# A conditional layer with a mixture of experts on one core: zero rows stored one unit later, row loads of single slots on another queue, and another order of one pair's sums

## The chip, the cores and the metric

The kernel is written for Trainium2 and runs on one core of one chip. A core has a matrix engine (TensorE, PE in the profile; PEld are its weight loads), a vector engine (VectorE, DVE), an engine for activation functions (ScalarE, ACT), a general engine (GpSimd, POOL) and a sequencer that here only issues transfers (SyncE, SP). Each engine works through its own instructions in program order and waits on semaphores for what others produce. Transfers (DMAs) are issued by SP, ACT and POOL; 16 DMA engines carry them out.

The metric is the device time of one execution in microseconds (us), lower is better. Before the change three runs gave 1175.25, 1177.22 and 1178.05 us, a median of 1177.22.

## The reference

Two layers with a residual each, all in float32. Eight blocks of 512 tokens (4 batches of 1024), 512 features.

```python
def _L0_cond_ref(Efou, y, weight):          # y: one condition vector per batch
    scale = 1.0 / np.sqrt(np.float32(weight.shape[0]))
    ys = y * scale
    d = rsqrt(einsum('bi,io->bo', ys * ys, weight * weight) + EPS)
    return einsum('bsi,io->bso', Efou * ys[:, None, :], weight) * d[:, None, :]

def _L1_cond_ref(x, t_emb, router_W, router_bias, w1, w3, w2, W1e, W2e):
    D, HS, HE, E, K = (512, 1024, 512, 8, 2)
    shared = silu(xf @ w1) * (xf @ w3) @ w2
    s = sigmoid(concatenate([xf, tf], axis=-1) @ router_W)
    _, topk_idx = top_k(s + router_bias, K)
    s_sel = take_along_axis(s, topk_idx, axis=1)
    gates = s_sel / (s_sel.sum(axis=1) + 1e-09)
    combine = zeros((N, E)).at[arange(N)[:, None], topk_idx].add(gates)
    h = gelu(einsum('nc,ech->enh', xf, W1e), approximate=False)
    y = einsum('enh,ehc->enc', h, W2e)
    routed = einsum('ne,enc->nc', combine, y)
    return (shared + routed) / 3

x = x + _L0_cond_ref(x, cond, L0_weight)
x = x + _L1_cond_ref(x, cond, ...)
```

The kernel computes only the two experts that each token has chosen: 8192 pairs of a token and an expert.

## The kernel before

**First layer.** For each of the eight blocks the kernel multiplies by the modulated weights (L450), adds the residual, and stores the result x1 in HBM as rows (`turn_back`, L356, through `store_segments` on SP, L130). The stores of the last two blocks are the last transfers ahead of the second layer.

**Units of the second layer.** From there on work is a list of units that are run one after the other. Each unit first begins its own products, then in `rest` interleaves its further products with the second half (`parts`) of the unit before. The list holds:

- 24 units `Shared`: six blocks, four pairs of 128 hidden features each (`HU` is 4), for the shared network;
- 12 units `Double`: each handles two slots at once. A slot is 256 rows (`GS`) that all go to one expert; a pair of slots shares one expert's weights;
- 8 units `Slot`: single slots 24 to 31 (`SINGLE` is 24, `SURE` is 32). Behind them a `tc.Switch` (L1466) on the number of spare slots runs up to seven more single slots, from 32 on; in the run that is shown there are two;
- 8 units `Shared` for the last two blocks, beside which the experts' results are gathered and added to the output.

Most block products use a scheme with seven products instead of eight, which needs sums of blocks of both operands. VectorE makes these sums ahead of the products. `Double.sums_of_first` (L1022) makes four from the first expert matrix, called 1, 2, 7 and 4 by the product that uses them; `Double.sums_of_tokens` (L1000) makes those of the tokens, 3, 2, 1 and 4. A unit's products run in the order 1, 2, 6, 7, 5, 3, 4; product 6 takes weight sum 2 and token sum 2, product 7 takes weight sum 7 and token sum 3, product 5 weight sum 1 and token sum 1, product 3 weight sum 4, product 4 token sum 4.

**Tasks.** Work that isn't part of a unit's own chain hangs on a table, `tasks`: unit number `at` runs `tasks[2 * at]` after its value and gate have been multiplied, and `tasks[2 * at + 1]` at its end. The tasks that the change touches:

- `fill(i)` (L696): one DMA on SP that writes 768 rows of zeros into `x1s_d`, the HBM array of rows sorted by slot. 13 fills cover it. Two are appended to each of tasks 0 to 5 and one to task 6. Task 0 also holds `fetch_pairs(0)` (L687, L691), which loads the first block's rows of x1 into `base`; it is appended behind the two fills of that task.
- For the first `Double`: task `10 * HU + 6` makes its weight sums, task `10 * HU + 7` its token sums. Both are run by the last shared unit ahead of the pairs.

Routing runs on VectorE in tasks 3 to 9. From task 10 on POOL scatters token rows into `x1s_d` with indirect DMAs (L712); these need the zero rows to be there.

**Transfers of the slots.** Weights and rows of a slot come from HBM:

- `fetch_first(j)` (L964, issues at L968): expert matrix W1e of slot j as four DMAs of 256 KB on SP;
- `fetch_second(j)` (L970, issue at L972): W2e, one DMA of 1 MB on SP;
- `load_rows(j)` (L978): the slot's 256 token rows from `x1s_d` as four DMAs of 128 KB, through `load_segments` (L121, issues at L125), on SP. There are three buffers for rows, used in turn;
- `turn_rows(j)` (L985): transposes them on VectorE;
- results go to `ys_d`, from the pairs on SP (L1196), from the single slots on ACT (L1318).

In a single slot's `rest` SP gets, in this order: the row load of slot j + 3, then (behind the last part of slot j - 1, next to whose store on ACT it stands) the second matrix of slot j + 2, then the first matrix of slot j + 3. Single slots use three sets of weight buffers in turn.

SP therefore works through the stores of x1, the fills and base loads, then the weights, rows and stores of the pairs, and the weights and rows of the single slots, strictly in that order. POOL issues the indirect DMAs and the transfers of the last stage.

Of the kernel before, what the change touches and what calls it, by code (L numbers as in the profile page):

```python
# [30 lines left out]
ALU = mybir.AluOpType  # L31
# [5 lines left out]
GS = 256  # L37
# [8 lines left out]
def kernel(  # L46
# [14 lines left out]
    nc = tc.nc  # L61
# [16 lines left out]
    SINGLE = 2 * PAIRED  # L78
# [3 lines left out]
    early = NB - TAIL  # L82
# [30 lines left out]
    x1s_d = dram.tile([ROWS, D], FP, name="x1s_d")  # L113
# [7 lines left out]
    def load_segments(eng, tile_ap, dram_rows):  # L121

        v = dram_rows.rearrange("(q i) (g c) -> g i q c", i=Q, c=P)
        for g in range(KC):
            eng.dma_start(out=tile_ap[ts(g, Q)], in_=v[g])  # L125
# [51 lines left out]
    HU, KH, TH = HSC // 2, KC // 2, TB // 2  # L177
# [32 lines left out]
    for _ in range(WARM // 2):  # L210
# [5 lines left out]
        out=ident4, in_=ident4, compare_op=ALU.not_equal, fill=1.0, base=0, pattern=[[-1, B]], channel_multiplier=1  # L216
# [4 lines left out]
    for k in range(KC):  # L221
        nc.gpsimd.affine_select(
            out=fold[ts(k, Q)],
            in_=fold[ts(k, Q)],
            compare_op=ALU.not_equal,
            fill=1.0,
# [15 lines left out]
    for _ in range(WARM - WARM // 2):  # L242
# [10 lines left out]
        out=before, in_=before, compare_op=ALU.is_ge, fill=1.0, base=0, pattern=[[-1, P]], channel_multiplier=1  # L253
# [148 lines left out]
    def token_sum(blk):  # L402

        b = x1T[blk]
        nc.vector.tensor_tensor(b[:, :KH, HI], b[:, KH:, HI], b[:, :KH, HI], ALU.subtract)
        begun.add(blk)

    def token_sums(blk):
        b = x1T[blk]
        k1, k2 = slice(0, KH), slice(KH, KC)  # L410
        v = t_tiles[blk % 2].rearrange("p (n k t) -> p n k t", n=3, k=KH)
        t1, t2, t4 = (v[:, n] for n in range(3))
        sub = lambda o, i0, i1: nc.vector.tensor_tensor(o, i0, i1, ALU.subtract)
        if blk not in begun:
            token_sum(blk)
        nc.vector.tensor_tensor(t2, b[:, k1, HI], b[:, k1, LO], ALU.add)
        sub(t1, b[:, k2, HI], t2)
        sub(t4, b[:, k2, LO], t2)
        t_of[blk] = (t1, t2, b[:, k1, HI], t4)
# [5 lines left out]
    def weight_sums(u, matrices=(0, 1)):  # L425
        for i in matrices:
            s1, s2, s4 = s_views(i, u)
            a11, a12, a21, a22 = (
                w13[i][:, k, ts(2 * u + m, P)] for m in range(2) for k in (slice(0, KH), slice(KH, KC))
            )  # L430
            nc.vector.tensor_tensor(s1, a21, a22, ALU.add)
            nc.vector.tensor_tensor(s2, s1, a11, ALU.subtract)
            nc.vector.tensor_tensor(a21, a11, a21, ALU.subtract)
            nc.vector.tensor_tensor(s4, a12, s2, ALU.subtract)
# [261 lines left out]
    def fill(i):  # L696

        rows_z = x1s_d[ds(i * FILL, FILL)].rearrange("(s p) d -> p s d", p=P)
        nc.sync.dma_start(out=rows_z, in_=zeros.unsqueeze(1).to_broadcast([P, FILL // P, D]))
# [31 lines left out]
    def out_sums(u):  # L731
        t1, t2, t4 = out_tiles(u)
        b1, b2 = w2_sb[:, 2 * u, :], w2_sb[:, 2 * u + 1, :]
        b11, b12, b21, b22 = b1[:, LO], b1[:, HI], b2[:, LO], b2[:, HI]
        if u not in summed:
            nc.vector.tensor_tensor(b12, b22, b12, ALU.subtract)
            summed.add(u)
        nc.vector.tensor_tensor(t2, b12, b11, ALU.add)
        nc.vector.tensor_tensor(t1, b22, t2, ALU.subtract)
        nc.vector.tensor_tensor(t4, b21, t2, ALU.subtract)  # L740
# [214 lines left out]
    weights, rows, xg = {}, {}, {}  # L955
# [8 lines left out]
    def fetch_first(j):  # L964
        ev = expert(j)
        va = w1e.rearrange("e (g k j) h -> e g j k h", g=KC, k=KC, j=Q)
        for g in range(KC):
            nc.sync.dma_start(out=weights[j][0][ts(g, Q)], in_=va[ds(ev, 1), g][0])  # L968

    def fetch_second(j):  # L970
        ev = expert(j)
        nc.sync.dma_start(out=weights[j][1], in_=w2e.rearrange("e (k p) d -> e p k d", p=P)[ds(ev, 1)][0])  # L972

    def fetch_weights(j):
        fetch_first(j)
        fetch_second(j)

    def load_rows(j):  # L978
        rows[j] = later["xseg"][j % 3]
        load_segments(nc.sync, rows[j], x1s_d[ts(j, GS)])  # L980

    def turn_rows(j):
        xg[j] = later["xg"][j % 2]
# [3 lines left out]
    def turn_half(j):  # L987

        x = big[early - 2 + j // 2 % 2]
        for k in range(KC):  # L990
            nc.vector.transpose(x[:, k, ts(j % 2, GS)], rows[j][:, :, ts(k, Q)])

    class Double:
# [25 lines left out]
            w = weights[2 * self.j][0].rearrange("p k (q m c) -> p k q m c", q=2, m=2)  # L1019
            return [w[:, k, :, m, :] for m in range(2) for k in (slice(0, KH), slice(KH, KC))]  # L1020

        def sums_of_first(self):  # L1022
            a11, a12, a21, a22 = self.blocks()
            s1, s2, s4 = later["s_w"]
            nc.vector.tensor_tensor(s1, a21, a22, ALU.add)
            nc.vector.tensor_tensor(s2, s1, a11, ALU.subtract)
            nc.vector.tensor_tensor(a21, a11, a21, ALU.subtract)
            nc.vector.tensor_tensor(s4, a12, s2, ALU.subtract)

        def halves_of_second(self):  # L1030
            w = weights[2 * self.j][1].rearrange("p (q m) d -> p q m d", q=2)
# [57 lines left out]
        def rest(self, prev, task):  # L1089
# [9 lines left out]
            if following:  # L1099
                turn_half(2 * j + 2)  # L1100
                load_rows(2 * j + 5)
            else:
                turn_rows(SINGLE)
# [4 lines left out]
            if following:  # L1108
                turn_half(2 * j + 3)
                load_rows(2 * j + 6)  # L1110
# [87 lines left out]
    class Slot:  # L1198
# [26 lines left out]
        def rest(self, prev, task):  # L1225
            parts = [lambda mm=mm, drain=drain: (mm(), drain()) for mm, drain in prev.parts()]
            parts[0]()
            self.stage1(1)
            if self.j + 1 < self.end:
                turn_rows(self.j + 1)  # L1230
            if self.j + 3 < self.end and self.j != SURE - 1:
                load_rows(self.j + 3)
            self.blocks()
            self.row_sum()
            parts[1]()
            self.stage1(2)
            parts[2]()
            self.weight_sums()
            self.stage1(3)
            parts[3]()  # L1240
            if self.j + 3 < self.end and self.j not in (SURE - 2, SURE - 1):
                fetch_first(self.j + 3)
            task(2 * self.at)
            task(2 * self.at + 1)
# [140 lines left out]
    units = [Shared(blk, u) for blk in range(early) for u in range(HU)]  # L1385
# [7 lines left out]
    tasks = {i: [] for i in range(2 * len(units))}  # L1393
# [9 lines left out]
    for u, work in (  # L1403
        (0, [lambda: out_sums(0)]),
        (1, [lambda: weight_sums(3, (0,))]),
        (2, [lambda: weight_sums(3, (1,)), lambda: out_sums(1)]),
        (3, [sigmoid, pick_first]),
        (4, [pick_second]),
        (5, [lambda: out_sums(2), count]),
        (6, [across, slots_of_experts]),  # L1410
        (7, [lambda: out_sums(3), positions]),
        (8, [load_spare, gates]),
        (9, [norm_gates]),
        (8 * HU + 1, [lambda: fetch_weights(0)]),
        (6 * HU + 4, [open_slot_pools]),
        (10 * HU + 1, [lambda: fetch_first(2)]),
        (10 * HU + 4, [lambda: fetch_second(2)]),
        (10 * HU + 4, [lambda: turn_half(0), lambda: load_rows(3)]),
        (10 * HU + 5, [lambda: turn_half(1), lambda: load_rows(4)]),
        (10 * HU + 6, [lambda: units[early * HU].sums_of_first()]),  # L1420
        (10 * HU + 7, [lambda: units[early * HU].sums_of_tokens((3, 2, 1, 4))]),
        (2 * late, [reload_last, lambda: out_sums(0)]),
        (2 * late + 1, [lambda: out_sums(1)]),
        (2 * late + 3, [lambda: out_sums(2)]),
        (2 * late + 6, [lambda: out_sums(3)]),
        (2 * late - 1, [lambda: token_sum(early)]),
        (2 * late + 3, [turn_last]),
        (2 * late + 5, [lambda: token_sums(last_blk)]),
        (2 * (late + HU + 1), [reload_w2]),
    ):  # L1430
        tasks[u] += work
    for i in range((NSLOT - SURE) * SUB):
        tasks[6 * HU + 4 + i].append(lambda i=i: clear_rows(i))
    for i in range(ROWS // FILL):
        tasks[i // 2].append(lambda i=i: fill(i))
    for m in range(NT // 2):
        tasks[9 + 2 * m].append(lambda m=m: stage_rows(m))
        for i in range(2):
# [98 lines left out]
```

## Time and profile before

| what | value |
|---|---|
| median of three runs | 1177.22 us (1175.25 to 1178.05) |
| profiled execution, its own time | 1177.57 us |
| its span, first to last instruction | 1175.8 us |
| mean granted TensorE clock | 0.994 |
| bytes moved by DMA | 203.65 MB, 173 GB/s over the span |
| SP's and ACT's queues (q1, q10) | 45.6% and 3.6% of the 16 DMA engines' span |
| POOL's queue (q0) | 10.7% |

The stages of the span, read from the timeline of each engine:

| from (us) | stage |
|---|---|
| 27 | first layer, PE without a gap until 144.5 |
| 151 | shared units of six blocks; fills on SP from 145.9 to 194.7, scatter on POOL from 252 to 532 |
| 581 | pairs of slots |
| 863 | single slots; the branch to the spare ones at 980 |
| 1022 | shared units of the last two blocks, gather on POOL from 1028.6 |

The groups of DMA issues that matter here (line, queue, number, size, median time from issue to landing):

```profile
big<-in_L_cond_W1e_dram SPq DMA_DIRECT2D x88, 256.0 KB, 5.6
big<-in_L_cond_W2e_dram SPq DMA_DIRECT2D x22, 1024.0 KB, 5.5
x1s_d<-w0t SPq DMA_DIRECT2D x13, 1536.0 KB, 15.7
xsegs<-x1s_d SPq DMA_DIRECT2D x136, 128.0 KB, 4.2
```

The first two are expert weights, the third the fills, the last the row loads of all 34 slots. A group's time to landing holds what the transfer waits for others in the same queue.

How to read the lines of the profile: `L968` is line 968 of the kernel; `out<-in` names the tiles that an instruction writes and reads, buffer numbers left out. In a timeline the first two numbers are start and duration in us, and brackets give the engine's idle time before and what ended it. In a table of waits the numbers are total us, how many, and the longest. `SPq` and `ACTq` are the sequencers of SP and ACT, where DMAs are issued. Who ended a wait is inferred from semaphores; a wait for several is put down to the one that came last.

### The profile page before, as it was taken

What the parts mean: (1) busy time and instruction counts of PE and PEld (TensorE: products, weight loads), DVE (VectorE), ACT (ScalarE), POOL (GpSimd) and SP (SyncE); (2) the same over time, 40 slices, a digit from 0 to 9 for tenths busy, and PEclk for the clock granted to TensorE, in tenths of its full rate; (3) what the DMA queues carried; (4) which work ended last, traced back from release to release, by engine and by line L of the source; (5) the groups of instructions that cost most, each with busy time, mean ns of one, the idle gap of its engine ahead of it and who ended that gap; (6) DMA issues with size and microseconds to landing.
All of it is one profiled execution on the core that took longest, in us unless ns stands there. A gap on an engine that the chain in (4) does not pass through costs nothing.

```text
span 1175.8 us, 14158 instructions
## 1 busy us (share of the span) xinstructions
PE 1147.1 (98%) x5078; PEld 947.8 (81%) x5078; DVE 715.9 (61%) x1484; ACT 219.2 (19%) x395; POOL 156.9 (13%) x180
## 2 busy tenths in 40 slices
PE   8999989999999999999999999999999998999998
PEld 6444578888888888888888888888888887888886
DVE  4547647855455454553786776767635453469987
ACT  2000022111111111111122222222222211121111
POOL 2000000012121121210000000000000000087750
PEclk9999989999999999999999999999999998999999
DMA  9598499133322446335256677556775898188971
GB/s 173 112 231 201 98 369 373 37 111 123 125 90 99 152 153 209 139 138 152 54 126 161 168 205 182 160 147 191 196 195 152 212 232 221 56 252 290 307 265 71
DMA packets 148335, 203.65 MB, mean 173 GB/s; under 512 B 9876, under 2 KB 77588, under 8 KB 148248
## 3 DMA queue, kind: packets, MB, share of 16 engines
q1 hardware_dynamic: 123960, 148.01, 45.6%
q0 software_dynamic: 12864, 41.99, 10.7%
q10 hardware_dynamic: 11424, 12.59, 3.6%
q8 instruction: 42, 0.69, 0.3%
q14 instruction: 45, 0.37, 0.1%
HBM read 120.76 MB, written 81.79 MB: 172 GB/s over the span
## 4 chain that ended last, share of the span: by engine, by line
PE 85%; DMA 5%; DVE 5%; issue 1%; SPq 1%; ACT 1%; ACTq 0%; DVEq 0%; POOLq 0%; POOL 0%
PE ch L774 17%; PE s L910 14%; PE d L1170 12%; PE pl L450 8%; PE se L774 8%; PE chd L1066 7%; PE ph L1215 4%; PE tw L774 4%; PE sed L1066 3%; PE yc L1273 2%; PE twd L1066 2%; DMA ys_d<-yr 2%; PE yo L1273 2%; DMA big<-in_L_cond_W1e_dram 1%; DMA seg<-in_x_dram 1%
## 5 line engine op out<-in xcount | busy, mean ns | idle before, releaser
L1342 POOL DMA_INDIRECT big<-ys_d,addr x64 | 70.5, 1102 | 522.3 <-DVE addr L1341 507.1
L926 DVE SCALAR_TENSOR_TENSOR base<-s,base 128x512 f32<-128x512 f32 x131 | 88.7, 687 | 78.4 <-PE s L910 74.8
L910 PE MATMUL s<-w_sb,hgh 128*128 128x256 f32 x496 | 122.7, 380 | 1.9 <-DVE base L926 1.9
L450 PE MATMUL pl<-xT,wm 128*128 128x512 f32 (+1 forms) x288 | 117.0, 554 | 1.5 <-DVE xT L280 1.4
L712 POOL DMA_INDIRECT x1s_d<-big,addr x64 | 64.5, 1008 | 360.6 <-DVE addr L711 339.5
L819 ACT ACTIVATE hgh<-ch 128x512 f32<-128x512 f32 x96 | 57.3, 597 | 284.6 <-PE ch L774 267.0
L910 PEld LDWEIGHTS s<-w_sb,hgh 128*128 128x128 f32 x496 | 93.8, 190 | 16.2 <-DVE base L926 3.5
L450 PEld LDWEIGHTS pl<-xT,wm 128*128 128x128 f32 x288 | 52.4, 190 | 52.8 <-issue 46.9
L823 DVE TENSOR_TENSOR hgh<-se,hgh 128x512 f32<-128x512 f32 x64 | 44.0, 688 | 77.4 <-ACT hgh L819 67.7
L910 PE MATMUL s<-more,hgh 128*128 128x256 f32 x316 | 81.3, 380 | 0.9 <-DVE xsegs L926 0.9
L774 PE MATMUL ch<-w0t,seg 128*128 128x256 f32 x256 | 62.8, 389 | 7.5 <-ACT hgh L819 7.4
L1187 DVE TENSOR_TENSOR yd<-d,yd 128x512 f32<-128x512 f32 x36 | 24.8, 689 | 71.1 <-ACT yd L1183 38.7
L910 PEld LDWEIGHTS s<-more,hgh 128*128 128x128 f32 x316 | 59.9, 190 | 9.6 <-DVE xsegs L926 1.3
L1170 PE MATMUL d<-big,hgh 128*128 128x256 f32 x288 | 66.1, 379 | 0.0
L774 PEld LDWEIGHTS ch<-w0t,seg 128*128 128x128 f32 x256 | 49.3, 194 | 15.9 <-ACT hgh L819 9.2
L1170 PEld LDWEIGHTS d<-big,hgh 128*128 128x128 f32 x288 | 54.7, 190 | 7.4
L774 PE MATMUL ch<-t,seg 128*128 128x256 f32 x256 | 60.5, 379 | 0.0
L774 PEld LDWEIGHTS ch<-t,seg 128*128 128x128 f32 x256 | 48.6, 190 | 6.6
L774 PE MATMUL ch<-big,w_sb 128*128 128x256 f32 x224 | 53.3, 381 | 0.0
L774 PE MATMUL se<-big,w_sb 128*128 128x256 f32 x224 | 53.0, 379 | 0.0
L774 PE MATMUL tw<-big,w_sb 128*128 128x256 f32 x224 | 52.9, 379 | 0.0
L774 PE MATMUL ch<-big,seg 128*128 128x256 f32 x224 | 52.9, 379 | 0.0
(263 smaller groups left out, 1934.6 us busy)
## 6 DMA issues: line engine op xcount, KB each, us to landing
big<-in_L_cond_W1e_dram SPq DMA_DIRECT2D x88, 256.0 KB, 5.6
big<-in_L_cond_W2e_dram SPq DMA_DIRECT2D x22, 1024.0 KB, 5.5
x1s_d<-w0t SPq DMA_DIRECT2D x13, 1536.0 KB, 15.7
xsegs<-x1s_d SPq DMA_DIRECT2D x136, 128.0 KB, 4.2
ys_d<-yd SPq DMA_DIRECT2D x24, 512.0 KB, 4.3
x_d<-back SPq DMA_DIRECT2D x32, 256.0 KB, 4.7
big<-x_d SPq DMA_DIRECT2D x16, 512.0 KB, 3.7
base<-x_d SPq DMA_DIRECT2D x12, 512.0 KB, 5.4
```

The source lines that it names most:

```text
L450: nc.tensor.matmul(pas[oc][:, ds(lo, n)], lhsT=wms[b][:, k, oc, :], rhs=xTs[blk][:, k, ds(lo, n)], start=(k == 0), stop=(k == KC - 1),)
L712: ins = nc.gpsimd.indirect_dma_start(out=x1s_d, out_offset=bass.IndirectOffsetOnAxis(ap=at.bitcast(U32), axis=0), in_=staged(t // 2)[:, t ...
L774: nc.tensor.matmul(out, lhsT=lhs[:, k, :], rhs=rhs[:, k, :], start=start and k == 0, stop=k == KH - 1, skip_group_check=not start,)
L819: nc.scalar.activation(self.both[:, :, m, cols], self.chain, AF.Copy)
L823: nc.vector.tensor_tensor(r, bank, r, ALU.add)
L910: nc.tensor.matmul(out[:, s], lhsT=a[:, ts(s, P)], rhs=b, start=start and s == 0, stop=True, skip_group_check=not (start and s == 0),)
L926: nc.vector.scalar_tensor_tensor(r, bank, third, r, ALU.mult, ALU.add)
L1066: nc.tensor.matmul(bank[:, q], lhsT=lhs[:, k, q, :], rhs=rhs[:, k, :], start=start and q == 0 and k == 0, stop=k == KH - 1, skip_group_che ...
L1170: nc.tensor.matmul(out[:, i], lhsT=a[:, q, ts(i, P)], rhs=b[:, q, :], start=start and i == 0 and q == 0, stop=q == 1, skip_group_check=not ...
L1215: nc.tensor.matmul(self.ph[:, i], lhsT=weights[j][0][:, k, ts(c, P)], rhs=xg[j][:, k, :], start=(k == 0), stop=(k == KC - 1),)
L1273: nc.tensor.matmul(out, lhsT=a[:, k, :], rhs=b[:, k, :], start=start and k == 0, stop=k == HC // 2 - 1, skip_group_check=not start,)
L1342: nc.gpsimd.indirect_dma_start(out=picks[t][i], out_offset=None, in_=ys_d, in_offset=bass.IndirectOffsetOnAxis(ap=at.bitcast(U32), axis=0) ...
```

## The change

Three things are changed.

1. `fill(i)` is appended to `tasks[1 + i // 2]` instead of `tasks[i // 2]`: every fill runs one task, half a unit, later. The first two now stand in task 1 and the last one in task 7.
2. `load_rows(j)` issues on SP for slots below `SINGLE` (24) and on GpSimd's queue for all others. The pairs' calls reach up to slot 26, so the loads of slots 24, 25 and 26, called from the last pairs, change their queue too.
3. `sums_of_first` takes the names of the sums that it makes. For the first pair, weight sums 1 and 2 stay in task 46; task 47 then makes token sums 3 and 2, weight sums 7 and 4, token sums 1 and 4. For the later pairs the call is as before.

```diff
     def load_rows(j):
         rows[j] = later["xseg"][j % 3]
-        load_segments(nc.sync, rows[j], x1s_d[ts(j, GS)])
+        load_segments(nc.sync if j < SINGLE else nc.gpsimd, rows[j], x1s_d[ts(j, GS)])
...
-        def sums_of_first(self):
+        def sums_of_first(self, names=(1, 2, 7, 4)):
             a11, a12, a21, a22 = self.blocks()
             s1, s2, s4 = later["s_w"]
-            nc.vector.tensor_tensor(s1, a21, a22, ALU.add)
-            nc.vector.tensor_tensor(s2, s1, a11, ALU.subtract)
-            nc.vector.tensor_tensor(a21, a11, a21, ALU.subtract)
-            nc.vector.tensor_tensor(s4, a12, s2, ALU.subtract)
+            for n, (out, i0, i1, op) in {
+                1: (s1, a21, a22, ALU.add),
+                2: (s2, s1, a11, ALU.subtract),
+                7: (a21, a11, a21, ALU.subtract),
+                4: (s4, a12, s2, ALU.subtract),
+            }.items():
+                if n in names:
+                    nc.vector.tensor_tensor(out, i0, i1, op)
...
-        (10 * HU + 6, [lambda: units[early * HU].sums_of_first()]),
-        (10 * HU + 7, [lambda: units[early * HU].sums_of_tokens((3, 2, 1, 4))]),
+        (10 * HU + 6, [lambda: units[early * HU].sums_of_first((1, 2))]),
+        (10 * HU + 7, [lambda: units[early * HU].sums_of_tokens((3, 2))]),
+        (10 * HU + 7, [lambda: units[early * HU].sums_of_first((7, 4))]),
+        (10 * HU + 7, [lambda: units[early * HU].sums_of_tokens((1, 4))]),
...
     for i in range(ROWS // FILL):
-        tasks[i // 2].append(lambda i=i: fill(i))
+        tasks[1 + i // 2].append(lambda i=i: fill(i))
```

## The prediction

> **What bounds the kernel now.** I read the page's first part, then a table by stage, then TensorE's (PE's) timeline, and last the waits of SyncE's queue (SP).
>
> ```profile
> PE 1147.1 (98%) x5078; PEld 947.8 (81%) x5078; DVE 715.9 (61%) x1484; ACT 219.2 (19%) x395; POOL 156.9 (13%) x180
> ```
>
> PE is the bound: the span is 1175.8 us, so only 28.7 us can be won without taking matmuls away. The table by stage says where they lie (us; PE, PEld, DVE, ACT and POOL busy, then granted clock, DMA share and GB/s):
>
> ```profile
> 145.00:241.00 96.00, 87.68 (x395) 75.98 (x396) 68.20 (x167) 20.19 (x35) 0.00 (x0) 0.96 0.70 254
> 575.00:610.00 35.00, 33.00 (x151) 28.05 (x150) 29.76 (x54) 7.65 (x12) 0.00 (x0) 1.00 0.21 62
> 925.00:955.00 30.00, 27.23 (x125) 23.40 (x124) 15.45 (x35) 5.46 (x12) 0.00 (x0) 1.00 0.91 225
> 955.00:985.00 30.00, 25.44 (x118) 22.00 (x116) 12.77 (x28) 5.46 (x12) 0.00 (x0) 0.99 0.92 239
> 985.00:1020.00 35.00, 33.78 (x141) 28.69 (x142) 14.56 (x32) 6.62 (x15) 0.00 (x0) 0.91 0.38 117
> ```
>
> The holes belong to the three places of the change: shared work begins at 145 (fills), pairs begin at 575 (their sums), single slots run from 888 to 1021 (row loads). PE's timeline has the five gaps, each in brackets with what ended it:
>
> ```profile
> 151.01 3.78 PE L774 MATMUL ch<-w0t,seg 128*128 128x256 f32 x8 [6.47 <-ACT hgh L819]
> 585.82 1.96 PE L1066 MATMUL chd<-t,more 128*128 128x256 f32 x8 [1.62 <-DVE t L1007]
> 926.90 1.97 PE L1215 MATMUL ph<-xg,big 128*128 128x256 f32 x8 [1.51 <-DMA big<-in_L_cond_W1e_dram]
> 954.30 1.97 PE L1215 MATMUL ph<-xg,big 128*128 128x256 f32 x8 [1.26 <-DMA big<-in_L_cond_W1e_dram]
> 985.47 3.75 PE L1215 MATMUL ph<-xg,big 128*128 128x256 f32 x8 [5.03 <-DMA xsegs<-x1s_d]
> ```
>
> Two gaps cost more than their length: behind 6.47 and 5.03 eight matmuls take 3.78 and 3.75 us, behind the others 1.96 to 1.97. The trace's clock record has half clock from 148.32 to 155.15 and from 984.59 to 991.42. So the second loses another (991.42 - 985.47) / 2 = 2.97 us.
>
> In the single stage the weights come late, and SP's waits (total, times, longest) say why:
>
> ```profile
> SPq L968 <- DMA ys_d<-yr: 44.3, 5, 12.7
> SPq L972 <- DMA ys_d<-yr: 9.3, 1, 9.3
> ```
>
> A fetch of expert weights waits for a *store of results* that ScalarE (ACT) issued, though the two share no data. The trace's instructions show the link: SP's and ACT's DMAs raise eight semaphores in turn (100, 102, 104 to 109), and each waits for the DMA before it on the same one. The fetch of 27, begun at 889.10, stood at its third part until 903.07, when slot 24's store on semaphore 100 had landed (issued 900.03, landed 903.05). DMAs were meanwhile idle:
>
> ```profile
> 895.00:901.00 6.00, 6.00 (x29) 5.29 (x28) 3.75 (x8) 1.36 (x3) 0.00 (x0) 1.00 0.03 10
> 910.00:913.00 3.00, 3.00 (x16) 2.64 (x15) 2.28 (x5) 0.98 (x2) 0.00 (x0) 1.00 0.00 0
> ```
>
> So this stage is short of issue, not of bandwidth.
>
> **Fills one unit later.** The same 13 transfers; the first two no longer stand at 145.93 and 147.30 behind the stores of x1, but behind the two base loads (150.19, 150.60). The first eviction (L819) waits for the last of those stores: issued 144.68, landed 150.11. Stores in that row land 1.0 to 1.4 us apart (125.45, 126.84, 128.01, 129.17 undisturbed; 146.79, 148.02 here), the last 2.09, the only one with fills behind it. Without them: 148.02 + 1.2 = 149.2, 0.9 us sooner. But half clock lasts to 155.15 either way, so each microsecond of it is worth half: **-0.4** (0 to -0.9). What is late next: the fills begin up to 4.2 us later, the last lands at some 210 instead of 206.45. SP's next issue behind them is at 217.94, the first scatter into the filled rows at 252.3; both cover it, and with that cover gone up to 4.2 us would show. The base rows land some 9 us sooner than 162.3; their first use is at 170.29: nothing.
>
> **Sums for the first pair.** Eight DVE operations in both versions, none added. Before: four weight sums (L1025 to L1028, 578.16 to 580.77), the add L823, the product L871, four hidden sums, then tokens 3 (584.27) and 2 (584.98); PE waits for the latter. After, sums 7 and 4, each 0.60 us of pitch (579.49, 580.09, 580.69), come behind tokens 2. All between moves up 1.2 us: L823 may run at 579.49, as its bank is done at 579.0; L871 follows ACT at some 580.9. PE starts at 584.6 instead of 585.82: **-1.2** (0 to -1.6, the whole gap). Late next are sum 7, ready at 585.1 where its product starts at 586.3, and sum 4 and tokens 1 and 4, done at 586.9 as before. PE has no hole from 600 to 925, so it keeps this.
>
> **Row loads of slots 24 and up on POOL.** 10 loads of four DMAs leave SP: 40 issues of 0.45 us, 18 us of a queue off the path. On POOL such a 128 KB load does not occur; the nearest are SP's own (0.45 us, landing in 3.7) and POOL's four loads of 256 KB at 1038 (0.66 us each, landing in 7 to 9), so 1.8 to 2.7 us a slot. POOL does nothing from 531 to 1028, which covers them: they wait for the turn of the slot three before, and the last (33, behind the turn at 956.9) is through by 960, ahead of the first gather at 1028.64. The rows are needed two slots, 26 us, later, so 9 us to land is hidden; without that cover a turn of 1.42 us would be late. POOL now passes the branch on the number of spare slots at 960, not 530; its 4.3 us there are hidden too.
>
> What counts is the order left behind. A slot now takes 6 of the eight semaphores' turns instead of 10, so a fetch shares one with a store further back. In a slot's own order the eighth after a store is a fetch more than a slot later; even if stores keep their present place, some 14 of SP's DMAs early, a fetch waits for the store of the slot three before it. That one meets idle DMAs and lands in 3 us; the last of four 256 KB parts lands 1.5 + 4.6 us later (issue, median landing). At 9 of the 13 us between slots (900.03, 912.98), both gaps close: **-2.8** (0 to -3.1 with their restarts).
>
> The third gap is another thing, whatever the row says of a row load. PE's sequencer meets the branch at 978.19 and has its next instruction 6.8 us later, having run dry at 980.44; SP, DVE and ACT need 6.1 to 6.8 too, with DMAs full (share 1.0 to 1.25). POOL took 4.3 at 530, DVE 2.8 at the branch's end at 1022 (share 0.05, then 0.49). With the row load of 33 and the weights of 32 gone from that moment (2.3 MB were issued from 975.5 to 980), but the fetch of 33 now likely there, I take 4.8 us, nearer POOL's: the gap falls from 5.0 to 3.0. Half clock began 4.1 us into this gap and 3.8 into the first, so a gap of 3.0 ends before it: -2.0 - 3.0 = **-5.0** (0, fetch as slow as now, to -8.0, all of it). The Trainium skill, "TensorE: Matmul & The Clock Gate", Part 1, states a free-running idle window of about 3.4 us; by it too 3.0 us keeps the clock, but 3.5 may not, and the term would be near -1.5. No run here shows a gap of that size.
>
> Sum: -0.4 - 1.2 - 2.8 - 5.0 = -9.4 on the profiled execution's 1177.57 us (span 1175.8 and 1.8 around it): **1168.2 us**. That execution is 0.35 above the median of 1177.22, inside the runs' own spread of 2.8.
>
> **Rivals.** *The branch stays as slow*: the sum without its last term, 1173.2. For it: the fetch of 33 now reaches the branch's moment. Against: it is 1 MB, less than what lies there now.
>
> *The queue brings nothing*: fetches still stand behind stores, or the DMAs are simply full (share 0.92 at 955). Only the first two terms: 1176.0. Against: shares of 0.03 and 0.00 while SP waited. The Trainium skill, "DMA: Bandwidth & Descriptors", "Issuing engines are not separate DMA queues", speaks for it: another issuing engine saves the sequencer's time alone; by that rule the result is this rival's 1176.0. The trace disagrees in so far as SP lost 53.6 us to those two rows of waits.
>
> *Slower: the store lands late at every slot.* If fetches still wait for the store of three slots before, and the DMAs are full when it is issued, it needs the 7.5 to 8.0 us seen from 925.93 on; then 8.0 + 1.5 + 4.6 = 14.1 against 13.0: 1.1 us late at each of seven slots, 7.9 instead of 2.8. 1177.57 + 5.1 - 1.6 = 1181.1. It decides once a store takes over 6.9 us to land. Against: the rows are what made that moment full.
>
> *Better*: the branch's gap and half clock vanish: 1165.2.
>
> **How the numbers follow.** Forecast 0.46, slow branch 0.26, nothing 0.10, slower 0.11, better 0.07. The measurement tells about 0.2%, 2.4 us. Forecast, slow branch and better are faster by more, and so 0.79; nothing lies within it, 0.10; slower 0.11. The range from 1164.5 to 1176.5 takes in the bounds of the branch's term and the rival that brings nothing, and leaves out the slower one and a little below.
>
> **What would show it.** The first matmul at L774 after the stores some 0.9 us sooner; the wait at L1007 down to 0.4; no waits of L968 or L972 for ys_d stores over some 4 us, and no gap ended by a W1e load in the single slots; PE's gap at the branch near 3 us and only one stretch of half clock. It is wrong if the fetches of 27 to 33 still stand for 8 to 13 us, if the branch's gap stays at 5 us, or if POOL's row loads end a wait of DVE.

## The result and the profile after

| | before | after |
|---|---|---|
| median (five runs each) | 1176.28 us | 1167.09 us |
| lowest and highest | 1175.25, 1178.05 | 1166.89, 1170.75 |
| profiled execution, its span | 1177.57, 1175.8 | 1166.89, 1165.1 |

The ratio of the times is 0.9929, with a 95% interval from 0.9911 to 0.9947: between 6 and 10 us faster. The forecast was 1168.2 us.

Where the time came from is seen in the same views as before. First the busy time of each engine, from the first part of the page of the kernel after:

```profile
PE 1143.6 (98%) x5078; PEld 946.0 (81%) x5078; DVE 715.7 (61%) x1484; ACT 219.2 (19%) x395; POOL 181.3 (16%) x220
```

PE has the same 5078 matmuls and 3.5 us less busy time, which is half clock gone. POOL has 40 instructions more, the row loads. The table by stage (length; busy PE, PEld, DVE, ACT, POOL; then granted clock, DMA share, GB/s), at roughly the places that correspond:

```profile
143.30:239.30 96.00, 88.41 (x406) 76.67 (x405) 68.45 (x168) 20.19 (x35) 0.00 (x0) 0.96 0.71 258
573.00:608.00 35.00, 34.20 (x157) 29.10 (x156) 30.57 (x55) 7.98 (x13) 0.00 (x0) 1.00 0.23 69
893.00:923.00 30.00, 30.00 (x140) 26.41 (x139) 15.96 (x35) 6.83 (x15) 4.61 (x8) 1.00 0.92 239
923.00:953.00 30.00, 30.00 (x140) 26.41 (x139) 16.75 (x39) 5.84 (x13) 4.61 (x8) 1.00 0.93 245
950.00:980.00 30.00, 27.06 (x126) 23.54 (x125) 13.12 (x30) 5.46 (x12) 0.00 (x0) 1.00 0.77 222
974.00:1009.00 35.00, 31.32 (x144) 26.61 (x142) 15.39 (x34) 6.71 (x16) 0.00 (x0) 1.00 0.23 78
```

The first of the three rows for the single slots has its counterpart in this row of the kernel before:

```profile
895.00:925.00 30.00, 30.00 (x140) 26.41 (x139) 15.73 (x34) 6.83 (x15) 0.00 (x0) 1.00 0.55 140
```

PE is now busy for all of 923 to 953, where it had 27.23 of 30 us; the row from 950 on holds the gap at the branch, and has 27.06 where it had 25.44. The DMAs' share in the three stretches was 0.55, 0.91 and 0.92 and is now 0.92, 0.93 and 0.77: the transfers come earlier, and less of them is left for the branch. From the branch on (974) the clock is 1.00 instead of 0.91. PE's timeline has three of the five gaps left:

```profile
150.03 3.53 PE L774 MATMUL ch<-w0t,seg 128*128 128x256 f32 x8 [5.26 <-ACT hgh L819]
583.17 1.97 PE L1070 MATMUL chd<-t,more 128*128 128x256 f32 x8 [0.41 <-DVE t L1007]
977.48 1.97 PE L1219 MATMUL ph<-xg,big 128*128 128x256 f32 x8 [2.94 <-issue]
```

Both gaps that ended with a W1e load are gone. The first has shrunk by 1.21 us, the second by 1.21, the one at the branch by 2.09, and its eight matmuls take 1.97 us instead of 3.75. Up to the last two microseconds of the span the clock record has one stretch of half clock, from 146.34 to 153.17. Added up: 1.2 (first gap) + 0.5 (half clock behind it, which cost (155.15 - 151.01) / 2 = 2.07 us and now (153.17 - 150.03) / 2 = 1.57) + 1.2 + 2.8 (two W1e gaps) + 2.1 + 3.0 (branch and its half clock) = 10.8 us. The spans differ by 10.7.

SP's waits in the single slots, from 886 to 986 us (total, times, longest):

```profile
SPq L968 <- DMA ys_d<-yr: 26.3, 4, 7.5
SPq L972 <- PE yc L1277: 25.5, 7, 8.8
```

Fetches still wait for stores, half as long, and the other wait is for the buffer that PE frees, as it should be. So something of the old order is left, and the runs below had to show whether it costs anything.

### The profile page after: what moved, and what is told of

Its sections match the earlier page's. It is cut to its first block, busy times and chain, and to the rows that moved or that the text cites. A ratio compares the mean times of both kernels' runs of the same rounds, so it can differ in the third digit from the quotient of the medians.

```text
span 1165.1 us, 14183 instructions
## 1 busy us (share of the span) xinstructions
PE 1143.6 (98%) x5078; PEld 946.0 (81%) x5078; DVE 715.7 (61%) x1484; ACT 219.2 (19%) x395; POOL 181.3 (16%) x220
## 5 line engine op out<-in xcount | busy, mean ns | idle before, releaser
L125 POOL DMA_DIRECT2D xsegs<-x1s_d x40 | 23.2, 588 | 388.3 <-DVE big L991 296.5
```

## The experiments

Three runs make one part of the change each. The others test the mechanism behind the third part, then what is left.

**One part at a time.** Fills alone:

```diff
-        tasks[i // 2].append(lambda i=i: fill(i))
+        tasks[1 + i // 2].append(lambda i=i: fill(i))
```

> The kernel before with the fills one unit later and nothing else. Theory (the last store of x1 lands sooner, half clock eats half of it): that store lands some 1.0 us sooner, the gap before the first eviction falls from 6.47 to 5.3 to 5.5 us, time 0.4 to 1.7 us below the kernel before, the branch's gap stays near 5 us. Rival (the fills' late end costs something before the scatter): a wait for a fill appears near 250 us and the time is not lower.

Measured 1175.82 us against 1177.27, ratio 0.9986 (0.9977 to 0.9994): 0.7 to 2.7 us, 1.6 in the middle, more than the 0.4 of the forecast. The first gap in the timeline of this kernel:

```profile
150.13 3.78 PE L774 MATMUL ch<-w0t,seg 128*128 128x256 f32 x8 [5.68 <-ACT hgh L819]
```

PE starts 0.88 us sooner, because the last store of x1 landed at 149.23 instead of 150.11, as worked out. The last fill landed at 208.23 and no instruction waited for one. The half clock here lasted from 145.89 to 156.13; it does not end "at 155.15 either way".

Sums alone (`sums_of_first` as in the diff of the change, and its two calls):

```diff
-        (10 * HU + 6, [lambda: units[early * HU].sums_of_first()]),
-        (10 * HU + 7, [lambda: units[early * HU].sums_of_tokens((3, 2, 1, 4))]),
+        (10 * HU + 6, [lambda: units[early * HU].sums_of_first((1, 2))]),
+        (10 * HU + 7, [lambda: units[early * HU].sums_of_tokens((3, 2))]),
+        (10 * HU + 7, [lambda: units[early * HU].sums_of_first((7, 4))]),
+        (10 * HU + 7, [lambda: units[early * HU].sums_of_tokens((1, 4))]),
```

> The kernel before with the new order of the first pair's sums alone. Theory: PE's gap at the first product with token sum 2 (1.62 us before) falls to 0.4, time 1.2 us below, nothing else moves. Rival (the four sums pushed back stop a later product): a new gap of up to 1 us within the first pair, time within 0.4 us of the kernel before.

Measured 1174.85 us, ratio 0.9981 (0.9973 to 0.9990): 1.2 to 3.2 us. Two lines of its timeline:

```profile
584.33 1.97 PE L1070 MATMUL chd<-t,more 128*128 128x256 f32 x8 [0.42 <-DVE t L1007]
926.04 1.97 PE L1219 MATMUL ph<-xg,big 128*128 128x256 f32 x8 [2.13 <-DMA big<-in_L_cond_W1e_dram]
```

The gap is the 0.42 us of the whole change; the W1e gaps stay, the first even longer than before (2.13). The gap accounts for 1.2 of the 2.2 us in the middle of that interval. In the profiled execution more was won at the branch, which this part does not touch: a gap of 4.58 us and half clock of 3.41 us behind it, against 5.03 and 6.83 before. The fills' execution had 4.66 and 3.41 there. The branch of the kernel before thus differs from one execution to the next by itself.

Row loads alone:

```diff
-        load_segments(nc.sync, rows[j], x1s_d[ts(j, GS)])
+        load_segments(nc.sync if j < SINGLE else nc.gpsimd, rows[j], x1s_d[ts(j, GS)])
```

> The kernel before with the row loads of slots 24 and up on GpSimd's queue alone. Theory: this part carries most of the change. Both gaps that a first-matrix fetch ended (1.51 and 1.26 us) go, the branch's gap falls from 5.0 to about 3 and its half clock goes: 7 to 8.5 us below the kernel before. Rival (the branch's time is chance and does not follow the load on the DMAs): only 2.8 us below, with the branch at 5 us and half clock behind it.

Measured 1170.66 us, ratio 0.9943 (0.9931 to 0.9956): 5.2 to 8.1 us, most of the whole. No W1e gap is left. Of the branch's gap a larger part stays than after:

```profile
981.06 3.54 PE L1215 MATMUL ph<-xg,big 128*128 128x256 f32 x8 [3.95 <-issue]
```

Behind it there is half clock for 3.41 us (980.85 to 984.27). Before had 6.83, but the fills alone and the sums alone had 3.41 there too, so this is not shown to come from the row loads.

In the middle of their intervals the three parts add up to 1.6 + 2.2 + 6.7 = 10.5 us; the whole change brought 8.4 (6.2 to 10.5). Within these errors they agree.

**Is it the shared semaphores, or the row loads' bytes and issues?** This kernel is the one before, with the row loads left on SP. Only the ten stores of the single slots change their queue, from ACT's to POOL's:

```diff
-            nc.scalar.dma_start(out=as_pair(ys_d, j * GS), in_=self.pair)
+            nc.gpsimd.dma_start(out=as_pair(ys_d, j * GS), in_=self.pair)
```

> The kernel before, its row loads still on SP, but the stores of the single slots' results on GpSimd's queue instead of ScalarE's. The same bytes, and SP issues as much as before. Theory (a fetch stands behind a store because both raise the same eight semaphores in turn): SP's waits for stores of results, 53.6 us in the single slots, vanish, both gaps ended by a first-matrix fetch (2.8 us) close, and the time falls by 2.8 us or more, up to 7.8 if the branch also gets quicker. Rival (the row loads on SP themselves, by their issue time or their bytes, make the weights late): both gaps stay and the time is within 1 us of the kernel before.

Measured 1170.02 us, ratio 0.9937 (0.9924 to 0.9949), as much as the row loads' move brings. Its SP waits, then SP's timeline at the fetch of 28 with the row load behind it:

```profile
SPq L972 <- PE yc L1273: 31.9, 7, 5.9
SPq L125 <- DMA big<-in_L_cond_W2e_dram: 7.1, 5, 2.1
```

```profile
900.45 1.99 SPq L968 DMA_DIRECT2D big<-in_L_cond_W1e_dram  x4
902.54 3.90 SPq L125 DMA_DIRECT2D xsegs<-x1s_d  x4
```

No wait for a store of a single slot (ys_d<-yr) is left. SP still issues every row load, 2.9 to 3.9 us of its time per slot, and the same bytes are moved; yet the fetch of 28, which began at 917.09 before, is out at 902.44, and both W1e gaps are gone. What cost the time was that a fetch stood behind a store on the same semaphore, not the row loads themselves. The branch's gap came down too, to 2.91 us: SP issues the last row load ahead of the branch, which before stood at 976.97 to 978.82, at 954.23 to 957.14 here.

**What the waits that are left cost.** The same edit on the kernel after:

> The changed kernel with the stores of the single slots on GpSimd's queue too. In the changed kernel SP's fetches still wait 26.3 us for stores of results, but no gap of PE is left that a fetch ended. Theory (those waits are now hidden, only the semaphores' sharing makes them): they vanish, and the time stays within 2 us of the changed kernel, 9 us below the kernel before. Rival (the late fetches still cost something at the branch, because they lie on the DMAs there): the branch's gap falls from 2.9 to 1.5 us or less, time 1 to 3 us below the changed kernel.

Measured 1168.30 us (1166.45 to 1170.8), ratio 0.9923 (0.9908 to 0.9938): no different from after, 0.9929. Its SP waits in the single slots, and PE's gap at the branch:

```profile
SPq L972 <- PE yc L1277: 51.9, 7, 9.0
```

```profile
978.45 1.96 PE L1219 MATMUL ph<-xg,big 128*128 128x256 f32 x8 [2.63 <-issue]
```

The 26.3 us of waits for stores have turned into waits for the buffer (25.5 to 51.9), and the time stayed: they were hidden.

**What makes the branch slow.** The forecast's largest term rests on a reading that the trace shows only by its coincidence: the branch takes longer when the DMAs are busy. So the kernel after gets a transfer of 2 MB that nobody reads, issued as PE comes to the branch:

```diff
+    junk_d = dram.tile([P, KC * HS], FP, name="junk_d")
...
+            if self.j == SURE - 1:
+                nc.scalar.dma_start(out=junk_d, in_=w13[0].rearrange("p k h -> p (k h)"))
```

> The changed kernel with an added transfer that nothing reads: 2 MB of a shared weight matrix stored to a scratch array from ScalarE's queue in slot 31, shortly before the branch. Theory (the engines' code for the branch is fetched over the same DMAs, so its time follows the load): PE's sequencer needs 6 to 7 us at the branch instead of 4.6, PE's gap grows from 2.9 to 4.5 to 5.5 us, half clock returns behind it, time 3 to 6 us above the changed kernel. Rival (the branch's time is chance or fixed): it stays at 4.5 to 5.7 us, time within 1.5 us of the changed kernel.

Measured 1171.80 us (1171.25 to 1173.44), ratio 0.9955 (0.9940 to 0.9971), and all its runs lie above after's. That is 4.7 us above after's median, or 3 us when each is compared with the runs of the kernel before taken beside it (0.9955 and 0.9929; the intervals just overlap), so the reading rests on the profile more than on the time. The store was issued at 971.82 and landed at 981.19. The branch instruction of PE's sequencer (name, duration in ns least/median/most, start) in after, then here:

```profile
L1538 PEldq COMPARE_BRANCH  x1: 4612/4612/4612, 972.3 to 972.3; - x1
```

```profile
L1541 PEldq COMPARE_BRANCH  x1: 6801/6801/6801, 973.0 to 973.0; - x1
```

```profile
980.26 3.49 PE L1220 MATMUL ph<-xg,big 128*128 128x256 f32 x8 [5.04 <-issue]
```

Before had 6786 ns and a gap of 5.03 us; with the transfer alone both are back, 6801 ns and 5.04 us, and half clock with them (980.53 to 983.94). So the DMA load sets the branch's time, and thinning it there is what the row loads' move gave, as the stores' move did.

The traces also hold how. Queue q8, one of the two that the page calls `instruction`, carries 42 or 43 packets of 16 KB in a whole execution, and in each of the ten kernels exactly one of them starts during PE's branch. It starts 3.74 us after the branch's start in before, 1.81 in after, 4.26 with the added transfer, and 1.37 to 3.51 in the other seven. From its start to the branch's end it is 2.5 to 3.1 us every time. What changes is therefore how long this packet, in all likelihood the code behind the branch, waits for the DMAs. The other engines' branches are not much quicker in after (SP, DVE and ACT 5.9 to 6.2 us), but PE did not wait for them.

**Something better: the first gap.** The largest gap left (5.26 us) waits for the last stores of x1. The kernel after stores them sooner: in the last block, the four chunks of the block before go out with the first two steps instead of one with each of four.

```diff
-                turn_back(blk - 1, [oc])
+                if blk < NB - 1:
+                    turn_back(blk - 1, [oc])
+                elif oc < 2:
+                    turn_back(blk - 1, [2 * oc, 2 * oc + 1])
```

> The changed kernel, but in the first layer's last block the rows of block 6 are turned back in the first two steps of four, two columns each, so that their stores leave some 6 us earlier and block 7's stores find the DMAs free. The same operations. Theory (the first eviction waits for the last store of x1 alone): that store lands near 144 instead of 149.1, PE's gap of 5.3 us falls below 1, its half clock goes; 5 to 7 us below the changed kernel. Rival (another wait stands right behind that store, or VectorE, busier in the first two steps, delays the first layer): the gap stays over 3 us or moves into the first layer, time within 2 us of the changed kernel.

Measured 1163.58 us (1161.15 to 1165.49), ratio 0.9877 (0.9859 to 0.9894). All its runs lie below all of after's; it beats both kernels. Its two gaps:

```profile
146.34 1.99 PE L777 MATMUL ch<-w0t,seg 128*128 128x256 f32 x8 [1.55 <-ACT hgh L822]
...
972.28 3.75 PE L1222 MATMUL ph<-xg,big 128*128 128x256 f32 x8 [2.97 <-issue]
```

The last store of x1 landed at 145.43 instead of 149.12, and no half clock follows. The gap is not below 1 as expected: the last four stores need until then to land. The branch's gap is no longer than in after, 2.97 against 2.94, but this time half clock followed it (971.45 to 978.28), which lost (978.28 - 972.28) / 2 = 3.0 us. The spans close: 3.7 + 1.6 - 3.0 = 2.3, and 1165.1 - 1162.8 = 2.3.

Both edits on after, the early turn and the stores on POOL's queue:

> The changed kernel with both edits: rows of block 6 turned back early, and the single slots' stores on GpSimd's queue. The two act 800 us apart, so their differences should add within 1.5 us: 14 to 17 us below the kernel before if the early turn does what its theory says, 9 to 11 if it does not.

Measured 1162.09 us (1160.61 to 1163.94), ratio 0.9864 (0.9849 to 0.9879). That is the lowest median of all, but its runs overlap with those of the early turn alone, and the stores' move brought nothing on after, so that only the early turn's gain is shown. In this profile half clock followed both gaps:

```profile
146.23 3.08 PE L777 MATMUL ch<-w0t,seg 128*128 128x256 f32 x8 [1.58 <-ACT hgh L822]
...
973.46 3.43 PE L1222 MATMUL ph<-xg,big 128*128 128x256 f32 x8 [2.56 <-issue]
```

## Why the prediction was right, step by step

**Fills: mechanism right, size too small.** The last store landed 0.9 us sooner, as forecast (alone 149.23, in the whole change 149.12), and the later fills delayed nothing. Mis-sized was the term of -0.4: it measured -1.6 (0.7 to 2.7). The step that failed is "half clock lasts to 155.15 either way, so each microsecond of it is worth half". The end differs from one execution to the next: 155.15 before, 153.17 after, 156.13 with the fills alone. If the end has no fixed place, a start 0.9 us sooner is worth 0.9 us on average; this is argued, and the interval holds it. What lies above 0.9 in the 1.6 no run explains; the interval does not tell the two apart.

**Sums: right.** Forecast -1.2; the gap went from 1.62 to 0.41 us in the whole change and to 0.42 alone. The time of the run alone fell by more (1.2 to 3.2 us), which the gap does not explain. Nothing behind it came late: the pairs of slots from 600 on still have no gap.

**Two W1e gaps: right in size, not right in why the margin holds.** Both went, -2.8, and the store's move alone took them away as well, which shows that the shared semaphores were the cause. But two steps of the working did not hold. "That one meets idle DMAs and lands in 3 us": the stores that a fetch waited for took 5.6 to 7.8 us (issued 949.18, landed 957.01), and so waits of up to 7.5 us stayed where none over 4 was forecast. And "a fetch waits for the store of the slot three before it" became four: the fetch of 28 was released by the store of 24 (landed 903.34), 30 by 26, 31 by 27, 32 by 28. SP's timeline of after at the fetches of 28, 30 and 32:

```profile
903.36 1.85 SPq L968 DMA_DIRECT2D big<-in_L_cond_W1e_dram  x4
...
923.09 8.72 SPq L968 DMA_DIRECT2D big<-in_L_cond_W1e_dram  x4
...
948.98 9.38 SPq L968 DMA_DIRECT2D big<-in_L_cond_W1e_dram  x4
```

Weights 28 landed by 911.56 and PE used them at 922.58; weights 30 stood 6.8 us within those 8.72, landed by 936.66 and were used at 948.48; weights 32 stood 7.5 us, landed by 962.61 and were used at 977.48; the tightest, 31, landed 10.3 us ahead of use. One slot, 13 us, more of room covered stores twice as slow as I had taken. For the same reason the slower rival did not come: its point, a store over 6.9 us to land, was passed (7.1 and 7.8), yet its 14.1 us were counted from the wrong store. Nor did the sign come that POOL's row loads end a wait of DVE: they took 0.58 us an issue, 2.3 us a slot, landed in 4.0 to 8.2 us, and nothing waited for one.

**The branch: size right, the clock by luck.** Forecast 4.8 us for the branch and a gap of 3.0; measured 4.61 and 2.94. That the DMA load makes the difference is shown by the added transfer. That 4.8 came so close is in part luck: POOL's 4.3 us at 530, which it leaned on, were taken with the DMAs full (share 0.98 to 1.09 from 530 to 534.4), and so gave no price for a thinner load. "Half clock began 4.1 us into this gap and 3.8 into the first, so a gap of 3.0 ends before it" came true in this execution but not as a rule. Half clock began 1.57 us into the first gap of this same trace, and 2.14 and 2.11 us into the branch's gaps of the two kernels with the early turn. At the branch, gaps of 2.94, 2.91 (stores on POOL, before) and 2.63 us (stores on POOL, after) kept the clock; 2.97 (early turn) and 2.56 (both edits) lost it. The Trainium skill, "TensorE: Matmul & The Clock Gate", Part 1, gives a free-running idle window of about 3.4 us; the trace agrees with windows of that length, but not with one that must be idle throughout, as no gap of 2.56 us holds 3.4. The term of -5.0 measured -5.1 in the profiled execution, of which the 3.0 for the clock do not come in every run: by the same working, the clock behind this branch cost 1.7 us in the execution of the fills alone and 1.5 in that of the sums alone. The runs of after lie in two groups, 1166.89 to 1167.09 and 1169.51 to 1170.75, some 3 us apart as that loss would be. Their granted clock was 0.996 to 0.997 and 0.995; that it is this loss at the branch was not traced.

**The rivals.** The branch that stays slow is what the added transfer makes: 1171.80, near the 1173.2 worked out. "The queue brings nothing" fell with the row loads alone at 0.9943. The Trainium skill, "DMA: Bandwidth & Descriptors", "Issuing engines are not separate DMA queues", says that DMAs run on the same 16 DMA engines whoever issues them, and that issuing on several engines saves only sequencer time. The trace agrees in so far as the fullest stretch of the single slots had a share of 0.92 before and 0.93 after. What the move gave here was not bandwidth but waits, 53.6 us of them before, 26.3 after, none with the stores moved too.

**What stays open.** The gap of 1.55 us at the first stores and the one at the branch are not removed in any version, and which runs lose the clock at the branch is not foreseen by anything seen here.

## What to carry to other kernels

When a DMA's issue waits for a transfer with which it shares no data, look which semaphore it raises and who raised it last: two queues that take turns on one set couple a fetch to another engine's store, and moving either of them to a third queue takes the coupling away. A wait that stays in the table costs nothing while its transfer lands ahead of use, so compare landing with use before removing it. Keep large transfers away from the moment of a branch, and value a gap of 2 to 3 us by several runs, since one execution may show it with half clock and the next without.

## What the runs showed that was not expected

Half clock comes in multiples of one length: 3.41 us (behind the branch with the rows alone and the added transfer, behind both gaps with both edits), 6.83 (before, after, early turn) and 10.24 (first gap of the fills alone), one, two and three times 3.41. Only a last stretch, cut off by the end of the record, differs. Full clock fits it too: after has 1010.35 us of it from 153.17 to 1163.51, 296 times 3.413. The granted clock thus changes on a grid of 3.41 us, and where a gap falls on it differs between executions.

Where the clock dropped at a branch's short gap, PE had been idle for about 2.1 us of the 3.41 up to that edge (2.14 with the early turn, 2.11 with both edits). Where it held, PE had been idle for 1.24 and 1.70 us of the two stretches that the gap touched (after), and for at most 1.52 and 1.60 with the stores on POOL's queue (on the kernel before and on after). A gap of 2.9 us may be cut in two halves by an edge or lie within one stretch, and that would explain why equal gaps end differently there; it rests on five gaps and was not tested by itself. It gives no threshold for the whole kernel: ahead of the first gap's half clock PE had been idle for only 1.43 us of the stretch (fills alone), 1.57 (after) and 1.58 (both edits), less than the 1.89 us of a stretch at the branch with the added transfer that kept the clock. Why the two places differ no run shows.

PE's branch took 4.2 to 4.7 us where the DMAs' share during it was 0.72 to 0.80, 5.70 with the row loads alone (1.04), and 6.3 to 6.8 in the other four (1.01 to 1.12).
